# Layer 0 with row pairs in four classes: 32 x 64 products for two row pairs at once, and mirrored edges without VectorE's shuffles

## The chip, the cores and the metric

The kernel is one launch on one NeuronCore of a Trainium2 chip. The metric is the device time of that launch in microseconds (us); lower is better. Times of single executions are from the hardware profiler. The engines are called TensorE (PE; its weight loads are listed as PEld), VectorE (DVE), ScalarE (ACT), GpSimd (POOL) and SyncE (SP); an engine's name with a q is its instruction queue, which also issues transfers (DMAs).

## What is computed

Four layers follow one another on an f32 input x of 4 images x 16 channels x 512 x 512. Each is `x = x + conv(groupnorm(x))`. Only layer 0 is changed. Cut to what matters:

```python
def block(x, w1, b1, w2, b2, w3, b3, a, b, c):
    # each channel t with its neighbours t-1, t+1 (mirrored at the ends) as 3 input planes
    trip = stack([x[:, prev], x, x[:, nxt]], axis=2).reshape(B * T, 3, H, W)
    o = a * conv_reflect(trip, w1, b1, dil=1, pad=2) \
      + b * conv_reflect(trip, w2, b2, dil=2, pad=4) \
      + c * conv_reflect(trip, w3, b3, dil=4, pad=8)      # 5 x 5 taps each, reflected edges
    return tanh(o).reshape(B, T, H, W)

x = x + block(block(groupnorm(x), blk1...), blk2...)      # layer 0
```

So layer 0 convolves twice, and each convolution reaches 8 rows and 8 columns in every direction. Layers 1 (3 x 3 convolution on quantised data), 2 (17 x 17 box filter) and 3 (a complex 3 x 3 convolution between two Fourier transforms) read what layer 0 leaves in a DRAM tensor x1, in the same layout before and after the change.

## The kernel before

**Work in groups and slots.** Layer 0 walks through 32 groups: 4 images x 2 convolutions x 4 groups of 4 frames (a frame is one channel of one image, in the layout of a convolution's input). The three input planes of four frames are combined as in a fast convolution along the channels: `early` and `late` (lines 488 to 525) form six combinations of six neighbouring frames, each multiplied with its own set of weights, and `gather` puts six products together into four outputs. One product set is one *slot*: 32 x 6 = 192 slots. `slot` (line 684) writes out the order of the work by hand, for every engine: in slot p TensorE computes product set p, VectorE and ScalarE gather set p-1, form later combinations, apply tanh and finish earlier frames, and SyncE issues the transfers (`transfers`, line 212: the loads of y first, then other loads, then stores, spread over the slot by marks on the products). `later` puts a step into a later slot. The engines work through their own instructions in the order in which `slot` emits them.

**Layout.** A frame is a tile of 128 partitions x 2376 elements. A partition holds a pixel position of 16 columns x 2 rows within a block of the image; the free axis runs over blocks of columns and over row pairs. A product contracts 32 partitions (2 rows x 16 columns) to 32 outputs (again 2 x 16). A tap that reaches other rows is a shift by a number of row pairs, from -4 to 4; `DELTA` lists the seven that occur. Two blocks of columns (e = 0, 1) reach all columns. So there are 7 x 2 = 14 products per output, summed in PSUM.

**`products` (line 529).** For each of the 14 it makes 16 calls, one for each 32 x 32 tile of the array (i: the 32 partitions that are contracted; j: the 32 PSUM partitions that are written), 512 columns each. The moving operand is 8 blocks x 64 consecutive row pairs, shifted by `DELTA`. PSUM has two tiles of 4 banks: while one set is computed, the other is read by `gather`.

**Frames.** `x_frame` (line 412) normalises x on ScalarE and transposes it in 32 x 32 blocks on VectorE. `activated` (line 602) writes the tanh of the first convolution to a tile y, with mirrored edge rows made by a ScalarE multiplication with a parity mask (line 622) and a VectorE sum (in `y_out`, line 625); `y_out` stores y to DRAM. `y_frame` (line 427) loads it again as a frame for the second convolution, in 16 transfers, and one slot later `mirror` swaps rows of the first and last column block with two VectorE shuffles over partitions (lines 449 and 450). `early` and `late` read the frame afterwards. `z_out` (line 636) transposes the second convolution's result, adds it to x, takes the maximum and the minimum of each partition (lines 648 and 651; layer 1 needs them) and stores x1. The sums for the next normalisation are ScalarE's (line 668). At an image's end ScalarE issues the stores of x1 itself (line 664).

**Weights.** `load_weights` (line 199) loads a new set of weights on ScalarE's queue when the convolution changes. A set has 14 blocks of 32 columns in the order of `DELTA`; the host arranges them by `DELTA` too.

Of the kernel before, what the change touches and what calls it, by code (L numbers as in the profile page):

```python
# [20 lines left out]
P = 128  # L21
# [7 lines left out]
PX = 32  # L29
DIL = (1, 2, 4)  # L30
DELTA = (-4, -2, -1, 0, 1, 2, 4)
# [89 lines left out]
class Layer0:  # L121
# [101 lines left out]
    def load_x(self, b, t, half, name):  # L223

        xt = self.pools["x"].tile([P, 2 * W], F32, name=f"{name}_{b}_{t}_{half}", tag="x")
        self.load_half(xt, b, t, half)
        return xt
# [184 lines left out]
    def x_frame(self, b, t, raws, ek, f):  # L412

        nc = self.nc
        fr = self.free.pop(0)
        v = fr.rearrange("p (k r) -> p k r", r=72)
        scale, bias, _ = self.gn[b]
        for h in range(2):
            raw = raws[h].rearrange("p (s w) -> p s w", s=2)
            xp = self.normalised(raw, scale[:, t : t + 1], bias[:, t : t + 1], f"{b}_{t}_{h}")  # L420
            nc.vector.transpose(v[:, :, 4 + h : 68 : 2], xp)  # L421
        rim = ek.rearrange("p k (e f m) -> p k e f m", e=2, f=4)
        for side in range(2):
            nc.scalar.copy(v[:, :, 68 * side : 68 * side + 4], rim[:, :, side, f, :])
        return fr

    def y_frame(self, t):

        nc = self.nc
        fr = self.free.pop(0)  # L430
        v, y = fr.rearrange("p (k r) -> p k r", r=264), self.y[t, :, :, 0:528]
        first, last = y[:, 0, 0:264], y[:, 3, 264:528]
        for c in range(4):
            at = PX * c
            lo, hi = slice(at, at + 16), slice(at + 16, at + PX)
            for to, src in ((v[lo, 1:9], y[hi]), (v[hi, 0:8], y[lo])):
                self.move(to.rearrange("p (a k) r -> p a (k r)", k=2), src, "first")
            if c > 0:
                self.move(v[lo, 0], last[at - 16 : at], "first")
            if c < 3:  # L440
                self.move(v[hi, 8], first[at + PX : at + PX + 16], "first")

        self.move(v[0:9:8, 0], first[16:25:8], "first")
        self.move(v[119:P:8, 8], last[103:112:8], "first")
        left = [16 + p + 8 - 2 * (p % 8) if p < 16 and p % 8 else p for p in range(PX)]
        right = [p - 16 + 6 - 2 * (p % 8) if p >= 16 and p % 8 < 7 else p for p in range(PX)]

        def mirror():
            nc.vector.stream_shuffle(v[0:PX, 0], v[0:PX, 0], left)
            nc.vector.stream_shuffle(v[96:P, 8], v[96:P, 8], right)  # L450

        self.later(1, mirror)
        return fr
# [5 lines left out]
    def fetch(self, gr, p):  # L459

        b, conv, g = gr["b"], gr["conv"], gr["g"]
        if g == 0:
            order = {0: (1, 2), 1: (4,), 2: (3,), 4: (5,)} if conv else {0: (1,), 1: (2,), 2: (4,), 3: (3,), 4: (5,)}
        else:
            order = {0: (2,), 1: (4,), 2: (3,), 4: (5,)} if conv else {0: (2,), 1: (4,), 2: (3,), 4: (5,)}
        for i in order.get(p, ()):
            if g == 3 and i == 5:
                continue
            t = 4 * g - 1 + i
            if conv:  # L470
                gr["d"][i] = self.y_frame(t)
                continue
            t0 = 0 if i == 1 else min(4 * g + 1, 12)
            rim = (self.rims_ahead.pop(t0, None) or self.load_rims(b, t0)) if i < 3 else None
            raws = None if (b, t) in self.held else [self.load_x(b, t, h, "xr") for h in range(2)]
            self.later(1, partial(self.made, gr, i, t, t0, rim, raws))
# [52 lines left out]
    def products(self, gr, p):  # L529
        nc, conv, q = self.nc, gr["conv"], ORDER[p]  # L530
        ps = self.psum.tile([P, 4, 512], F32, name=f"m{self.now}", tag="m")
        v = gr["v"][q].rearrange("p (k r) -> p k r", r=264 if conv else 72)
        w = self.w[q].rearrange("p (n o) -> p n o", o=PX)
        for n in range(NPB):
            e, dr = n // len(DELTA), DELTA[n % len(DELTA)]
            for turn in range(16):
                i, j = turn // 4, turn % 4
                rows = slice(PX * i, PX * i + PX)
                r0 = 4 + dr + (64 * j if conv else 0)
                k0 = e + (0 if conv else 8 * j)  # L540
                ins = nc.tensor.matmul(  # L541
                    ps[PX * j : PX * j + PX, i, :].rearrange("p (k r) -> p k r", r=64),
                    w[rows, n],
                    v[rows, k0 : k0 + 8, r0 : r0 + 64],
                    start=(n == 0),
                    stop=(n == NPB - 1),
                    skip_group_check=True,
                )
            self.marks.append(ins.ins)
        gr["m"][q] = ps  # L550

    def gather(self, gr, p):
# [9 lines left out]
        def part(h):  # L562

            if conv:
                return m.rearrange("p c (k r) -> p (c k) r", r=64)[:, :, h::2]
# [36 lines left out]
    def activated(self, gr, i, h, src):  # L602
# [8 lines left out]
        else:  # L611
            if h == 0:
                gr["out"][i, 0] = self.pools["rb"].tile([P, 8, 264], F32, name=f"y_{name}", tag="rb")
            z = gr["out"][i, 0]
            o = z[:, :, 4 + 128 * h : 132 + 128 * h].rearrange("p k (c r) -> p c k r", c=2)
            nc.scalar.activation(o, src.rearrange("p (c k r) -> p c k r", c=2, k=8), AF.Tanh, bias=bias)
            to, even, odd = (
                (z[:, :, 0:4], z[:, :, 8:4:-1], z[:, :, 7:3:-1])
                if h == 0
                else (z[:, :, 260:264], z[:, :, 259:255:-1], z[:, :, 258:254:-1])  # L620
            )
            nc.scalar.mul(to, even, self.parity[:, 0:1])
            gr["rim"].append((to, odd))

    def y_out(self, gr, i):
        nc = self.nc
        for to, odd in gr["rim"]:
            self.stt(to, odd, self.parity[:, 1:2], to)
        gr["rim"].clear()
        y = self.y[4 * gr["g"] + i, :, :, 0:528]  # L630
        z = gr["out"].pop((i, 0)).rearrange("p (a k) r -> p a (k r)", k=2)
        wait = 2 if i == 3 else 1
        for a in range(4):
            self.later(wait, partial(self.move, y[:, a], z[:, a], "stores"))

    def z_out(self, gr, i):
# [8 lines left out]
        def finish():  # L645
            for h in range(2):
# [4 lines left out]
                nc.vector.tensor_reduce(self.low[:, b, t, h : h + 1], xs[h], AX.X, ALU.min)  # L651
# [5 lines left out]
        def leave():  # L657
            to = self.x1[b, :, t, :].rearrange("(p T s) w -> T p s w", T=2, s=2)
            neg = self.gn[b][2][:, t // 2 : t // 2 + 1]
            junk = self.pools["sum"].tile([P, 1024], F32, name=f"junk_{b}_{t}", tag="E")  # L660
            for h in range(2):
                x = xs[h].rearrange("p (s w) -> p s w", s=2)
                if self.last_of_image:
                    nc.scalar.dma_start(to[h], x)
                for r in () if self.last_of_image else range(0, P, PX):
                    self.move(to[h][r : r + PX], x[r : r + PX], "stores")
# [17 lines left out]
    def slot(self, n, p):  # L684
# [22 lines left out]
        if cur:  # L707
            self.products(cur, p)
        if done:
# [28 lines left out]
    def begin(self, gr):  # L738
# [3 lines left out]
        else:  # L742
            self.y = scratch(self.k.dram, f"y_{b}", [C, P, 4, 536])

    def run(self):
        self.groups = [
            {"b": b, "conv": conv, "g": g, "d": {}, "v": {}, "m": {}, "out": {}, "rim": [], "xb": {}}
# [989 lines left out]
```

## Time and profile before

| | us |
|---|---|
| device time, three runs | 5312.73, 5320.9, 5336.15 (median 5320.9) |
| profiled execution, its span from the first instruction to the last | 5311.8 |
| layer 0 in it (first product at 61.1, last one at 3019.9) | 2959 |

The page gives no other time of the profiled execution than its span; the fastest of the three runs lies 0.9 us above it.

| engine | busy us | share of the span |
|---|---|---|
| PE | 5017.0 | 94% |
| PEld | 3644.6 | 69% |
| DVE | 4034.8 | 76% |
| ACT | 2490.1 | 47% |
| POOL | 6.9 | 0% |

How to read the profile: a group of instructions stands as line, engine, operation, output<-inputs, partitions x elements and count; then, after the bar, busy time in us and mean ns of one; then the idle time of the engine just before them and what ended most of it. Matmuls are pipelined, so their durations overlap, and their ends are modelled; the distance between their starts tells more than the duration. A stretch is a window of the span, in us from its start.

### The profile page before, as it was taken

How to read it: one execution, taken by the hardware profiler on the slowest of the kernel's cores; microseconds unless marked ns; L12 is line 12 of the kernel's file. 1: busy time of each engine (PE TensorE's matmuls, PEld its weight loads, DVE VectorE, ACT ScalarE, POOL GpSimd, SP SyncE). 2: the span in 40 equal slices, each digit the busy share in tenths (PEclk: the TensorE clock that was granted, in tenths of full speed). 3: DMA queues.
4: the chain of work that ended last, by engine and by line, in shares of the span. 5: the costliest groups of instructions: out<-in, count | busy, mean ns of one | idle time of the engine just before them, and what ended most of it. 6: DMA issues, size and time to landing. Idle time of an engine off the chain costs nothing.

```text
span 5311.8 us, 270483 instructions
## 1 busy us (share of the span) xinstructions
PE 5017.0 (94%) x125040; PEld 3644.6 (69%) x125040; DVE 4034.8 (76%) x4765; ACT 2490.1 (47%) x3955; POOL 6.9 (0%) x20
## 2 busy tenths in 40 slices
PE   5999998999999999989999799998999989999999
PEld 3766666866666766768767655656887867777776
DVE  8857989758988669887679865555555578888887
ACT  3533345543345533444123454544454446666665
POOL 0000000000000000000000000000000000000000
PEclk9999999999999999999999899999999989999999
DMA  6555555555545465543446477776766655555554
GB/s 187 160 145 154 145 153 152 158 150 141 139 148 169 140 164 138 148 133 120 107 121 158 130 225 226 237 222 203 232 215 205 215 158 143 144 149 149 144 143 120
DMA packets 445356, 861.49 MB, mean 162 GB/s; under 512 B 74304, under 2 KB 96704, under 8 KB 443968
## 3 DMA queue, kind: packets, MB, share of 16 engines
q1 hardware_dynamic: 417520, 800.16, 52.2%
q10 hardware_dynamic: 26704, 44.03, 2.5%
q8 instruction: 979, 16.04, 1.4%
q14 instruction: 153, 1.25, 0.1%
HBM read 503.87 MB, written 340.03 MB: 159 GB/s over the span
## 4 chain that ended last, share of the span: by engine, by line
PE 90%; DVE 5%; issue 3%; DMA 1%; ACT 1%; SPq 0%; ACTq 0%; POOL 0%; DVEq 0%; POOLq 0%
PE m L541 52%; PE l1p L992 10%; PE l2p L1099 8%; PE u L1567 4%; PE s L1508 4%; PE u L1508 4%; PE u L1530 2%; PE pt L1542 2%; DVE l2o L1139 2%; PE l2p L1150 1%; DVE st L1140 1%; PE pr L1552 0%; DVE frame L457 0%; SPq L208 0%; DMA l0w<-frame 0%
## 5 line engine op out<-in xcount | busy, mean ns | idle before, releaser
L541 PE MATMUL m<-frame,l0w 32*32 32x512 f32 x86016 | 2863.1, 605 | 157.4 <-issue 76.7
L541 PEld LDWEIGHTS m<-frame,l0w 32*32 32x32 f32 x86016 | 2069.1, 103 | 950.5 <-issue 366.6
L457 DVE SCALAR_TENSOR_TENSOR frame<-frame,frame 128x2376 f32<-128x2376 f32 x232 | 607.8, 2628 | 8.8 <-DMA x<-xb 0.6
L992 PE MATMUL l1p<-l1q,l_wt 32*32 32x512 f32 x12288 | 482.2, 599 | 71.3 <-DVE l1q L982 36.2
L992 PEld LDWEIGHTS l1p<-l1q,l_wt 32*32 32x32 f32 x12288 | 257.8, 103 | 241.7 <-issue 162.5
L1139 DVE TENSOR_TENSOR l2o<-l2x,l2p 128x512 f32<-128x512 f32 x256 | 172.8, 675 | 266.5 <-PE l2p L1099 266.5
L668 ACT ACTIVATE junk<-xb,neg 128x1024 f32<-128x1024 f32 x256 | 294.1, 1149 | 62.9 <-DMA l0w<-l0w 19.9
L1099 PEld LDWEIGHTS l2p<-k_c_band,l2y 128*128 128x128 f32 x2048 | 256.7, 190 | 75.8 <-issue 55.0
L1099 PE MATMUL l2p<-k_c_band,l2y 128*128 128x144 f32 (+1 forms) x2048 | 284.2, 292 | 6.1
L1128 ACT COPY l2y<-l2p 128x512 f32<-128x512 f32 x256 | 149.9, 586 | 283.3 <-PE l2p L1099 283.3
L1099 PE MATMUL l2p<-k_c_band,l2n 128*128 128x144 f32 (+1 forms) x2048 | 269.2, 292 | 14.1 <-ACT l2n L1117 10.7
L1099 PEld LDWEIGHTS l2p<-k_c_band,l2n 128*128 128x128 f32 x2048 | 262.7, 197 | 14.8 <-ACT l2n L1117 11.3
L1009 DVE BATCH_NORM_STATS2 l1st<-l1o 128x6 f32<-128x512 f32 x256 | 158.2, 681 | 140.0 <-ACT l1o L1007 140.0
L1007 ACT ACTIVATE l1o<-l1p,k_l_bias,l_osc 128x1024 f32<-128x1024 f32 x128 | 147.2, 1200 | 236.2 <-PE l1p L992 230.1
L1567 PE MATMUL u<-k_c_hil,zt 128*128 128x128 f32 x2048 | 255.9, 278 | 0.0
L574 ACT COPY C<-m 128x1024 f32<-128x1024 f32 x64 | 61.6, 1014 | 393.2 <-PE m L541 288.3
L1567 PEld LDWEIGHTS u<-k_c_hil,zt 128*128 128x128 f32 x2048 | 238.4, 192 | 2.1 <-issue 0.8
L421 DVE STREAM_TRANSPOSE frame<-xp 128x1056 f32<-128x1056 f32 x128 | 162.7, 1281 | 96.7 <-ACT xp L390 96.6
L1543 ACT COPY zt<-pt 128x512 f32<-128x512 f32 x256 | 131.4, 599 | 208.6 <-PE pt L1542 208.6
L1473 DVE TENSOR_TENSOR xc<-l3n,k_c_tab 128x2048 f32<-128x2048 f32 x64 | 146.7, 2293 | 107.2 <-ACT l3n L1457 107.2
L1586 DVE SCALAR_TENSOR_TENSOR l3o<-u,l3t 128x256 f32<-128x256 f32 x512 | 192.5, 427 | 22.2 <-ACT l3t L1578 19.5
L992 PE MATMUL l1p<-l1x,l_wt 32*32 32x512 f32 x4088 | 196.2, 597 | 0.0
(312 smaller groups left out, 6374.8 us busy)
## 6 DMA issues: line engine op xcount, KB each, us to landing
y<-y SPq DMA_DIRECT2D x256, 264.0 KB
frame<-y SPq DMA_DIRECT2D x512, 132.0 KB
x<-l1o SPq DMA_DIRECT2D x256, 256.0 KB
l2x<-x SPq DMA_DIRECT2D x64, 1024.0 KB
x<-l2o SPq DMA_DIRECT2D x64, 1024.0 KB
l3x<-x SPq DMA_DIRECT2D x256, 256.0 KB
out<-l3o SPq DMA_DIRECT2D x256, 256.0 KB
l1x<-x SPq DMA_DIRECT2D x252, 256.0 KB
```

Source lines behind the costliest of these rows:

```text
L421: nc.vector.transpose(v[:, :, 4 + h : 68 : 2], xp)
L457: self.nc.vector.scalar_tensor_tensor(o, x, f, y, ALU.mult, ALU.add)
L541: ins = nc.tensor.matmul(ps[PX * j : PX * j + PX, i, :].rearrange("p (k r) -> p k r", r=64), w[rows, n], v[rows, k0 : k0 + 8, r0 : r0 + 64 ...
L668: nc.scalar.activation(junk, xs[h], f, bias=neg, accum_out=self.out_sums[n][:, 2 * t + h : 2 * t + h + 1])
L992: ins = nc.tensor.matmul(ps[32 * j : 32 * j + 32, b, :], wt[rows, a, d], qs[v % 3][rows, k, d : d + W] if d < 3 else raws[v][rows, k], sta ...
L1009: nc.vector.bn_stats(st[b][:, u, :], o[:, b, :])
L1099: nc.tensor.matmul(ps[:, lo:hi], lhs[:, k, at : at + P], band[:, j : j + hi - lo], start=(k == 0), stop=(k == 3), skip_group_check=True,)
L1128: nc.scalar.copy(yts[i][:, wb, :], ps)
L1139: nc.vector.tensor_add(o[:, hb, :], xt[:, hb, :], ps)
L1508: nc.tensor.matmul(ps[b][32 * j : 32 * j + 32], f[rows, n, j, :], x[rows, j, :], start=(i == 0), stop=(i == 2 and tag == "s"), skip_group_ ...
L1567: nc.tensor.matmul(po[:, bass.ts(k, P)], zt[:, b, k ^ 1, :], hil[:, k, :], start=False, stop=(k == 3), skip_group_check=True,)
L1586: nc.vector.scalar_tensor_tensor(o[:, v].rearrange("p k u -> p u k"), po[:, HW:W].rearrange("p (u k) -> p u k", u=2), s, t.rearrange("p (u ...
```

## The change

1. **Products.** The row pairs of a frame are stored in four classes (a frame's row pairs are dealt out in turn) so that two neighbouring row pairs of the output can be computed by one call: 32 partitions are contracted to 64 outputs, with the weight blocks of two shifts side by side. `DELTA` is put in an order in which such pairs lie next to each other. Of the seven shifts, ten of fourteen uses per pair of outputs are made in five such wide calls (`PAIRS`); the other four are made in 32 x 32 calls as before (`ALONE`). Each slot has its wide calls in one run and its narrow ones in another, wide first in even slots and narrow first in odd ones. Per slot 80 + 64 = 144 calls stand where 224 stood. The moving operand is read in runs of 16 or 32 elements.
2. **Frames and y.** The transposes, copies and tanh write in the new order, and the DRAM scratch for y has a new layout; a y frame comes in 22 transfers instead of 16, a y store goes in four of 32 partitions with 8.4 KB each instead of four of 128 partitions with 2.1 KB each.
3. **Mirrored edges.** The two VectorE shuffles and the parity steps in `activated` and `y_out` go. The loads of y fetch mirrored column blocks. `mirror` now is six small ScalarE multiplications per y frame, one slot after the load, emitted right after the products and ahead of `gather` (`self.do("edges")`); four of them fill a small tile that VectorE adds to the frame later in the slot (`added`). A GpSimd memset clears the two edge columns of every y tile.
4. **The minimum** in `z_out` is a `tensor_scalar` with an accumulated minimum, written over zr, instead of a `tensor_reduce`.
5. **Transfers of xb and x1** go in four pieces of 32 partitions in the new order of rows, also where ScalarE issues one whole store now.

```diff
-DELTA = (-4, -2, -1, 0, 1, 2, 4)
+DELTA = (4, 2, 0, -2, -4, 1, -1)
+PAIRS = ((4, 0), (2, 1), (0, 2), (-2, 3), (1, 5))
+ALONE = (((-4, 4), (6, 0)), ((-1, 6), (3, 5)))
...
     def y_frame(...)
+        whole = self.y[t, :, :, 0 : 32 * 132].rearrange("u (h s j) (k n) -> h s j u k n", h=2, s=2, n=132)
+        y = whole[:, :, ::-1]
         for c in range(4):
...
+            first, last = 1 if c == 0 else 0, 8 if c == 3 else 9
+            for to, src in (
+                (v[lo, :, first:9], y[1, :, :, :, 8 * c - 1 + first : 8 * c + 8]),
+                (v[hi, :, 0:last], y[0, :, :, :, 8 * c : 8 * c + last]),
+            ):
+                for u in range(2):
+                    part = src[:, :, u].rearrange("s j k n -> s j (k n)")
+                    self.move(to[:, u].rearrange("p k n -> p (k n)"), part, "first")
...
         def mirror():
-            nc.vector.stream_shuffle(v[0:PX, 0], v[0:PX, 0], left)
-            nc.vector.stream_shuffle(v[96:P, 8], v[96:P, 8], right)
-        self.later(1, mirror)
+            for side, m, back in ((0, 1, odd), (65, 64, even)):
+                nc.scalar.mul(at(0, 0, side, 1188, 66), at(1, 1, m, -1188, -66), back)
+            nc.scalar.mul(edge[:, :, :, 0, 0], at(0, 0, 2, 1187), even)
+            nc.scalar.mul(edge[:, :, :, 0, 1], at(1, 1, 1, -1188), even)
+            nc.scalar.mul(edge[:, :, :, 1, 0], at(1, 0, 64, -1188), odd)
+            nc.scalar.mul(edge[:, :, :, 1, 1], at(0, 1, 64, 1187), odd)
+        def added():
+            to = fr.rearrange("p (n c m) -> p n c m", n=18, c=2)[:, :, :, 0:66:65]
+            nc.vector.tensor_add(to, to, edge.rearrange("p u k s c -> p (u k) c s"))
+        self.later(1, mirror, "edges")
+        self.later(1, added)
...
     def products(self, gr, p):
-        for n in range(NPB):
-            e, dr = n // len(DELTA), DELTA[n % len(DELTA)]
-            for turn in range(16):
-                i, j = turn // 4, turn % 4
-                ins = nc.tensor.matmul(ps[PX * j : PX * j + PX, i, :]..., w[rows, n], v[rows, k0 : k0 + 8, r0 : r0 + 64], ...)
+        runs = [(e, pair) for e in range(2) for pair in PAIRS], [(e, two) for e in range(2) for two in ALONE]
+        order = [(wide, *what) for wide in ((1, 0) if p % 2 == 0 else (0, 1)) for what in runs[1 - wide]]
+        for n, (wide, e, what) in enumerate(order):
+            base = len(DELTA) * PX * e
+            for i in range(4):
+                for j in range(2):
+                    if wide:
+                        d, o = what
+                        at = base + PX * o
+                        ins = product(slice(64 * j, 64 * j + 64), i, slice(at, at + 64), d, e, j, n)
+                        continue
+                    for u, (d, o) in enumerate(what):
+                        at = base + PX * o
+                        out = slice(64 * j + PX * u, 64 * j + PX * u + PX)
+                        ins = product(out, i, slice(at, at + PX), d, e, j, n)
...
     def activated(...)
+                nc.gpsimd.memset(gr["out"][i, 0][:, :, 0:66:65], 0.0)
...
-            nc.scalar.mul(to, even, self.parity[:, 0:1])
-            gr["rim"].append((to, odd))
     def y_out(self, gr, i):
-        for to, odd in gr["rim"]:
-            self.stt(to, odd, self.parity[:, 1:2], to)
...
     def z_out(...)
-                nc.vector.tensor_reduce(self.low[:, b, t, h : h + 1], xs[h], AX.X, ALU.min)
+                nc.vector.tensor_scalar(
+                    zr[:, h], x, 1.0, None, ALU.mult, ALU.min, accum_out=self.low[:, b, t, h : h + 1]
+                )
...
     def slot(self, n, p):
         if cur:
             self.products(cur, p)
+        self.do("edges")
         if done:
             self.gather(done, at)
```

`product` is the same matrix product call, with a moving operand of three levels: blocks, two classes, and 32 (second convolution) or 16 (first) row pairs of each class.

## The prediction

> **What bounds the kernel now.** I read the page first: the chain of work that ended last, then the costliest groups. The changed layer is the first 3020 of 5311.8 us, and the chain lies on TensorE.
>
> ```profile
> PE 90%; DVE 5%; issue 3%; DMA 1%; ACT 1%; SPq 0%; ACTq 0%; POOL 0%; DVEq 0%; POOLq 0%
> ...
> L541 PE MATMUL m<-frame,l0w 32*32 32x512 f32 x86016 | 2863.1, 605 | 157.4 <-issue 76.7
> L541 PEld LDWEIGHTS m<-frame,l0w 32*32 32x32 f32 x86016 | 2069.1, 103 | 950.5 <-issue 366.6
> ```
>
> The reader is to see that the products of layer 0 (L541) keep TensorE busy for 2863 us and that each of the 32 groups x 6 slots x 224 calls stands there twice (86016 = 192 x 448): an f32 product runs as two passes, each with its own weight load. Then I read the table of stretches for one image, cut at its eight groups (four of the first convolution, four of the second). Columns: stretch, length, busy time of PE, PEld, DVE, ACT and POOL, clock, DMA share, GB/s.
>
> ```profile
> 808.70:913.20 104.50, 93.52 (x2691) 64.83 (x2695) 98.36 (x90) 61.91 (x106) 0.00 (x0) 0.91 0.52 155
> 913.20:998.70 85.50, 85.50 (x2703) 73.50 (x2686) 70.23 (x55) 51.58 (x98) 0.00 (x0) 1.00 0.52 164
> 998.70:1084.60 85.90, 85.90 (x2708) 72.97 (x2689) 65.50 (x51) 48.74 (x87) 0.00 (x0) 1.00 0.47 146
> 1084.60:1179.20 94.60, 91.75 (x2707) 60.74 (x2697) 51.76 (x57) 30.86 (x50) 0.00 (x0) 1.00 0.61 153
> 1179.20:1269.70 90.50, 89.30 (x2706) 61.81 (x2687) 67.73 (x78) 24.60 (x33) 0.80 (x2) 1.00 0.54 148
> 1269.70:1362.90 93.20, 91.51 (x2704) 57.90 (x2690) 88.95 (x85) 33.47 (x45) 0.00 (x0) 1.00 0.60 145
> 1362.90:1453.40 90.50, 89.72 (x2715) 61.34 (x2694) 81.97 (x75) 31.27 (x44) 0.00 (x0) 1.00 0.52 136
> 1453.40:1552.30 98.90, 90.10 (x2704) 65.10 (x2687) 79.52 (x73) 46.34 (x80) 0.00 (x0) 0.99 0.51 154
> ```
>
> Stretches 2 and 3 are pure TensorE: 85.9 us for 6 x 448 pairs of load and matmul, 32 ns a pair, 14.3 us a slot. Stretch 1 and stretches 6 to 8 are held almost as much by VectorE (79.5 to 98.4 us busy). Stretch 4, where the first convolution hands over to the second, has both engines partly idle.
>
> **TensorE: the term that decides.** Per slot the change makes 10 wide products per 32 rows by 64 columns tile (80 calls on 8 tiles) and 4 narrow ones per 32 by 32 tile (64 calls on 16 tiles): 144 calls, 288 pairs, where 448 stood. The multiplications stay the same: each tile still streams 14 products of 512 columns. So the gain hangs on whether a pair or a stream is the limit. Today 14 rounds of 16 tiles take 14.3 us, 1.02 us a round. What a bare stream takes shows in layer 3, where L1530 works on two tiles of 64 rows, again 512 columns in f32 (timeline, start and length in us):
>
> ```profile
> 4426.45 1.59 PE L1508 MATMUL u<-xs,f 32*32 32x512 f32 x26
> 4427.97 1.99 PE L1530 MATMUL u<-cor,lc 64*128 64x512 f32 x8
> 4429.89 0.33 PE L1542 MATMUL pt<-k_c_ident,z 128*128 128x128 f32 x1
> ```
>
> Eight passes start over 1.40 us (1.99 less the 0.59 of the last one, the median of this line) with one 0.11 us of first weights in it: three steps of 0.43 us, two passes at a time. A product of two passes thus streams in 0.86 us, and its loads of 128 columns (186 ns each) are hidden. Layer 0 needs 1.02, so 0.16 us a round are not streaming. The likeliest cause is the number of pairs in flight: L1508 takes the same tiles in another order (four row blocks first, then the next column block) and starts 87 passes in the 3.00 us from 4421, 34 ns each, so the order of tiles matters little and the count of instructions much.
>
> Wide part: from below 10 x 0.86 = 8.6 us, the stream; from above 10 x 1.02 = 10.2, no gain. I take 8.6, because L1530 is the only row with tiles wider than 32 columns, and its loads were twice as long as 64 columns need. Narrow part: 4 x 1.02 = 4.1. New per slot: one change of tile shape. No such change stands between 32 by 32 and 32 by 64 in the trace; the nearest is L1508 to L1530 above, where the last start before lies 0.52 us ahead of the first after it and the first weights take 0.11 more. From below 0.1 (weights alone), from above 0.62; I take 0.35. Sum 8.6 + 4.1 + 0.35 = 13.05 us against 14.3: **1.2 us a slot, 7.2 us a group**, wherever TensorE alone is the limit. Ends: 8.6 + 4.1 + 0.1 saves 1.5; 10.2 + 4.1 + 0.62 costs 0.6. The moving data now come in runs of 16 or 32 elements rather than 64; L541's runs of 64 and L1508's of 512 go alike, so I cost that at 0.
>
> The Trainium skill speaks against this part twice. Its page TensorEngine Tiling (Array Packing), Key Properties, says that changing the tiling mode drains TensorE; it gives no figure. TensorE: Matmul & The Clock Gate, Part 3, says that a weight load overlaps running matmuls only where its row group differs; by that rule a wide tile's longer loads would stay exposed and the slot would keep its 14.3 us. L1530 differs: with two row groups, both always streaming, its loads cost nothing after the first, so the trace decides.
>
> **VectorE.** The rows it rests on:
>
> ```profile
> L651 DVE TENSOR_REDUCE low<-xb 128x1 f32<-128x1024 f32 x128 | 156.1, 1220 | 4.4
> ...
> L457 DVE SCALAR_TENSOR_TENSOR y<-y,k_c_parity 128x32 f32<-128x32 f32 x128 | 30.7, 249 | 180.7 <-ACT y L622 152.6 <-DMA xr<-in_x 14.6 <-DMA l0w<-l0w 12.4
> L450 DVE STREAM_SHUFFLE frame<-frame 32x264 f32<-32x264 f32 x64 | 29.0, 453 | 2.0
> L449 DVE STREAM_SHUFFLE frame<-frame 32x264 f32<-32x264 f32 x64 | 28.1, 440 | 0.8 <-issue 0.6
> ...
> L519 DVE TENSOR_SCALAR frame<-frame 128x2376 f32<-128x2376 f32 x8 | 11.1, 1390 | 0.0
> ```
>
> Gone: 128 shuffles (57.1 us) and 128 parity sums (30.7). New: 64 small additions of 128x72; the 128x64 product of L1491 took 225 ns, so 64 x 0.24 = 15. The minimum becomes a TENSOR_SCALAR that accumulates: as a plain one by L519 (1390 ns for 2376 elements) 0.60 us for 1024, plus the 82 ns read-out that L648 shows, 0.68; as slow as the reduction plus read-out, 1.30. I take 0.68, the same operation's row: 128 x 0.54 = 69 us less (other end: 10 more). In a second-convolution group that is 8 x 0.54 + 4 x 0.89 - 4 x 0.24 = **6.9 us** (1.9 at the other end); in a first-convolution group 8 x 0.25 = 2.0.
>
> **ScalarE, GpSimd, SyncE.** ScalarE gives up 128 multiplications of 325 ns (42 us) and takes 384 of 36 elements; L389's 128x16 took 206 ns and L622's 128x32 325, so 80 to 125 us, 1.2 to 2.0 us in a slot that loads a frame. It was busy 25 to 33 us of 90 in those groups, so the work itself costs nothing; if that cover were gone, it would be 80 us. Its place does matter: these now stand ahead of the PSUM copies and wait for the frame's loads (rival below). The 64 memsets on GpSimd (busy 6.9 us in all) stand before the first tanh, which waits for the same buffer anyway: 0, at most 0.2 us each by the 128x128 memset of L812. A y frame takes 22 transfers where 16 stood, 384 more on SyncE's queue; the 32 of two frames from 342.5 us took 25.1 us there, 0.78 each, for twice the bytes that most of the new ones carry. Bytes are the same and pieces longer (4.2 to 8.4 KB for 2.1). I cost it at nothing except in stretch 4, where that queue already runs behind. The stores of x1 and the loads of xb keep pieces of 4 KB and their number, but for the 64 whole stores that ScalarE issues at an image's end: they become 256 quarters. The one at 1499.64 us took 0.46 us to issue, so between 0 and 192 x 0.46 = 88 us, hidden in stretches 8 and 1, where ScalarE is busy 46 of 99 and 62 of 104 us.
>
> **The sum, by group of an image.** Stretches 2, 3 and 5 are TensorE's, VectorE stays below 71: 7.2 each. Stretch 4: half, 3.6, as transfers share it. Stretches 6 and 7: VectorE lets go of at most 6.9; I take 5 each. Stretch 8 ends in VectorE work: 4. Stretch 1 likewise: 3. Together 42.2 us; four images 169. 5311.8 - 169 = 5143 for the profiled execution. The three runs lie 0.9, 9.1 and 24.4 us above its span, the median 9.1, so **5150 us** for the median.
>
> **Rivals.** (a) TensorE gains, but it is given back: the low minimum stays at 1.30 us, stretches 6 and 7 give 1.5 each, 1 and 8 nothing, and stretch 4 nothing: 24.6 an image, 98; with some waits of ScalarE on loads 80: **5240**. For it: VectorE's 89 of 93.2 us in stretch 6.
>
> (b) The round of 1.02 us belongs to streaming 16 tiles' worth of output, not to the count of pairs. Then a slot is 14.3 + 0.35; stretches 2, 3 and 5 lose 2 each, 6 to 8 gain 1 to 2 from VectorE: about +2 an image, **5330**, no change. For it: nothing shows a 32 by 64 tile. Against it: L1530.
>
> (c) Slower: ScalarE waits. It runs in order, the mirrored edges now stand ahead of the copy of the finished products, and their loads can be late (waits in layer 0):
>
> ```profile
> DVE frame L449 <- DMA frame<-y: 113.2, 16, 10.5
> ```
>
> Today VectorE met this late in the slot, 16 times of 64. At the head of the slot ScalarE meets it 5 to 15 us sooner. The other half of PSUM gives TensorE one slot of patience, so it decides only where a load lands over about 11 us into the slot after the one that issued it; the two frames of stretch 4 do (their queue ran to 367.7, the slot began at 355.4). If every one of the 64 frames cost 4 us, 256 - 169 = 87: **5400**.
>
> **Chances.** Forecast 0.53; (a) 0.20; (b) 0.11; (c) 0.16. Range 5080 (1.5 us a slot and all 6.9 us of VectorE: 52 an image, 207; and 36% of the 77 us that PE waited on issue, 28, for 36% fewer instructions) to 5340, which takes in (a) and (b) and leaves out (c) and a little below: 0.8. A difference under 0.5% can't be told from no change here. Faster by over 0.5%: 0.53 + 0.20 - 0.01 = 0.72; within: 0.12; slower: 0.16.
>
> **What will show it.** Right: in stretches 2 and 3 a group of about 79 us with wide passes about 53 ns apart (8.6 us for 160), one gap under 0.6 us at each change of shape, the minimum at 0.68 us. Wrong: wide passes 64 ns apart (rival b), or ScalarE's copies of L574 waiting for frame<-y with TensorE idle behind them (c).

## The result, and the profile after it

The changed kernel takes 6271.31 us (median of 4 runs, 6269.15 to 6273.69), beside 5316.81 us (4 runs) of the kernel before: a ratio of 1.1793, 95% interval 1.1768 to 1.1818. It is **slower by 18%**. The forecast was 5150 us; 5340, the top of the range, is 930 us too low.

The page of the profiled execution (span 6271.9 us), first its chain of work that ended last, by engine, and then groups of instructions:

```profile
PE 63%; DMA 16%; DVE 10%; issue 4%; SPq 3%; ACT 3%; ACTq 0%; DVEq 0%; POOL 0%
...
L579 PE MATMUL m<-frame,l0w 32*64 32x512 f32 (+1 forms) x55296 | 2730.2, 636 | 1269.6 <-ACT C L626 579.7
L579 PEld LDWEIGHTS m<-frame,l0w 32*64 32x64 f32 (+1 forms) x55296 | 1173.4, 123 | 2825.5 <-issue 1635.4
L471 ACT ACTIVATE frame<-frame,k_c_parity 128x36 f32<-128x36 f32 x128 | 39.3, 355 | 1414.8 <-DMA frame<-y 523.2
```

Transfers hold 16% of the chain where they held 1%. The products have 55296 passes instead of 86016 and TensorE is busy with them for less time than before, but it idles 1269.6 us ahead of them instead of 157.4, and 924 us of that idle time end with a copy of ScalarE (L626, which empties a PSUM tile; 579.7 and 344.1 us for its two tiles). ScalarE in turn idles 1415 us ahead of its mirrored edges (L471); 523 of them, the largest part, are put down to loads of y, and 641 to transfers of xb and x1 that share the queue with them.

The table of stretches for the same image (stretch, length, busy time of PE, PEld, DVE, ACT and POOL with counts, clock, DMA share, GB/s):

```profile
1064.60:1180.30 115.70, 90.28 (x1735) 37.08 (x1743) 105.44 (x94) 63.25 (x107) 0.38 (x2) 0.86 0.49 142
1180.30:1270.60 90.30, 82.23 (x1736) 36.75 (x1728) 70.68 (x46) 45.54 (x78) 0.76 (x4) 0.94 0.48 148
1270.60:1362.80 92.20, 82.35 (x1741) 36.89 (x1732) 72.07 (x45) 47.21 (x82) 0.75 (x4) 0.93 0.44 139
1362.80:1524.60 161.80, 85.23 (x1737) 36.97 (x1729) 46.80 (x33) 33.59 (x65) 0.74 (x4) 0.77 0.23 78
1524.60:1684.60 160.00, 89.39 (x1739) 35.78 (x1731) 60.45 (x60) 30.64 (x56) 1.17 (x4) 0.77 0.24 83
1684.60:1821.80 137.20, 85.84 (x1736) 36.67 (x1728) 83.90 (x77) 37.68 (x68) 0.00 (x0) 0.80 0.32 100
1821.80:1954.50 132.70, 83.77 (x1736) 36.74 (x1728) 83.54 (x77) 39.54 (x70) 0.00 (x0) 0.82 0.35 105
1954.50:2065.50 111.00, 86.07 (x1737) 36.68 (x1721) 88.90 (x85) 47.79 (x81) 0.00 (x0) 0.90 0.48 135
```

The image takes 1000.9 us where it took 743.6. Of the 257 us that are lost, 223 are in stretches 4 to 7, which load the frames of y (stretches 2 to 5 store them): stretch 5 needs 160 us instead of 90.5. There no engine is busy for more than 90 us of 160, and the transfers move less, not more: 83 GB/s at a DMA share of 0.24, where 148 and 0.54 stood. So the time is lost to transfers that are slow without being many.

Where they are slow shows in SyncE's queue (timeline: start and length of a run of issues). First the kernel after, then the kernel before, each in its second convolution:

```profile
1698.34 23.18 SPq L219 DMA_DIRECT2D frame<-y  x22
1722.66 4.41 SPq L219 DMA_DIRECT2D x<-xb  x8
1727.16 23.09 SPq L219 DMA_DIRECT2D frame<-y  x22
```

```profile
1271.64 10.53 SPq L217 DMA_DIRECT2D frame<-y  x16
1282.28 5.66 SPq L217 DMA_DIRECT2D x<-xb  x8
1288.03 12.07 SPq L217 DMA_DIRECT2D frame<-y  x16
```

A frame here keeps the queue for 23 us instead of 11 to 12, for 22 transfers instead of 16. A product slot lasts 13 us. Over all 64 frames it is 22.8 to 31.9 us (24.9 in the middle), where it was 10.5 to 17.3 (12.3). ScalarE's row at the same place (timeline; in brackets the idle time and its releaser) shows what stands behind it:

```profile
1725.07 0.61 ACT L471 ACTIVATE frame<-frame,k_c_parity 128x36 f32<-128x36 f32 x2 [22.97 <-DMA frame<-y]
...
1726.44 1.90 ACT L626 COPY A<-m 128x1024 f32<-128x1024 f32 x2
```

The edges wait 23 us for the load, and the copy that frees PSUM waits behind them. The DMA columns of two windows of this kernel, one over loads of xb and one over the frame loads, say what kind of slowness it is:

```profile
1688.40:1698.20 9.80, 9.64 (x224) 3.94 (x208) 6.32 (x9) 6.88 (x12) 0.00 (x0) 1.00 0.74 193
1698.40:1721.40 23.00, 13.50 (x288) 5.62 (x288) 22.86 (x20) 3.63 (x6) 0.00 (x0) 0.88 0.17 59
```

At 0.17, fewer than 3 of the 16 DMA engines are at work. In the packet records of the second window packets of 4752 bytes take 184 ns each and run two at a time (16.7 of 17.5 us); the stores of y, packets of 8448 bytes, run four at a time (18.8 of 20.5 us from 1270). The diff has these numbers: a load of 16 rows is written as two steps of eight rows (`s j`, s = 2, because j is stored and read backwards, which leaves the mirrored pieces in plain order), a store of 32 rows as four steps of eight (`u q j n`, q = 4).

### The profile page after: what moved, and what is told of

Same layout as the page of the kernel before. It is cut to its first block, busy times and chain, and to the rows that moved or that the text cites. A ratio compares the mean times of both kernels' runs of the same rounds, so it can differ in the third digit from the quotient of the medians.

```text
span 6271.9 us, 210181 instructions
## 1 busy us (share of the span) xinstructions
PE 4879.1 (78%) x94320; PEld 2747.2 (44%) x94320; DVE 4064.1 (65%) x4573; ACT 2555.3 (41%) x4211; POOL 18.6 (0%) x84
## 4 chain that ended last, share of the span: by engine, by line
PE 63%; DMA 16%; DVE 10%; issue 4%; SPq 3%; ACT 3%; ACTq 0%; DVEq 0%; POOL 0%
PE m L579 31%; DMA frame<-y 12%; PE l1p L1037 9%; PE l2p L1144 6%; PE u L1612 4%; PE s L1553 4%; PE u L1553 3%; SPq L219 3%; PE u L1575 2%; PE pt L1587 2%; DVE frame L487 2%; DVE frame L428 1%; DVE l2o L1184 1%; DMA xr<-in_x 1%; PE l2p L1195 1%
## 5 line engine op out<-in xcount | busy, mean ns | idle before, releaser
L579 PE MATMUL m<-frame,l0w 32*64 32x512 f32 (+1 forms) x55296 | 2730.2, 636 | 1269.6 <-ACT C L626 579.7
L579 PEld LDWEIGHTS m<-frame,l0w 32*64 32x64 f32 (+1 forms) x55296 | 1173.4, 123 | 2825.5 <-issue 1635.4
L471 ACT ACTIVATE frame<-frame,k_c_parity 128x36 f32<-128x36 f32 x128 | 39.3, 355 | 1414.8 <-DMA frame<-y 523.2
L487 DVE SCALAR_TENSOR_TENSOR frame<-frame,frame 128x2376 f32<-128x2376 f32 x232 | 607.9, 2629 | 8.9 <-PE m L579 0.5
L479 DVE TENSOR_TENSOR frame<-frame,edge 128x72 f32<-128x72 f32 x64 | 15.9, 248 | 880.3 <-ACT edge L475 553.7
L428 DVE STREAM_TRANSPOSE frame<-xp 128x1056 f32<-128x1056 f32 x128 | 259.3, 2109 | 50.4 <-ACT xp L397 50.4
L691 DVE CUSTOM_DVE_ANT_0 xb<-xb,zr 128x1024 f32<-128x1024 f32 x128 | 156.2, 1220 | 140.3 <-DMA xb<-in_x 140.2
```

What stands on the lines that cost most here:

```text
L428: nc.vector.transpose(v[:, :, :, h, 1:17].rearrange("p k u m -> p k m u"), xp)
L487: self.nc.vector.scalar_tensor_tensor(o, x, f, y, ALU.mult, ALU.add)
L579: return nc.tensor.matmul(ps[at, i, :].rearrange("p (k c m) -> p k c m", k=nc_, c=2), w[PX * i : PX * i + PX, weights], source(i, d, e, j) ...
L691: nc.vector.tensor_tensor_reduce(x, x, zr[:, h], 1.0, -3.0e38, ALU.add, ALU.max, self.top[:, b, t, h : h + 1])
```

## The experiments

**Theory A**: a transfer runs on as many DMA engines as its outermost step has entries, 2 for the new loads and 4 for the new stores, and that is the loss. **Rival B** is the prediction's slower case: the loads are late anyway, and ScalarE's edges ahead of the copies make TensorE pay. **Rival C**: the new products or the layout in classes are slow. Each ratio below is to the kernel before as it ran on the same occasion (5295.63, 5313.76, 5317.45 or 5308.63 us); where runs of two occasions are compared, the difference by their ratios stands in brackets.

### The shape of the transfers

`e1_rows16` keeps products, frames and edges, and stores y with its rows in plain order, so that loads have one step of 16 rows and stores one of 32. The mirrored column blocks, for which the order was reversed, go to a small tensor ye of their own (four more small stores a frame; four of the 22 loads read it).

```diff
-        y = whole[:, :, ::-1]
+        y = whole
...
+        rows = self.y[t, :, :, 0 : 32 * 132].rearrange("u (h p) (k n) -> h p u k n", h=2, n=132)
...
-                    part = src[:, :, u].rearrange("s j k n -> s j (k n)")
+                    part = src[:, u].rearrange("p k n -> p (k n)")
...
-        y = self.y[4 * gr["g"] + i].rearrange("u (q j) n -> u q j n", j=8)[:, :, ::-1]
+        y = self.y[4 * gr["g"] + i]
...
+            to = self.ye[4 * gr["g"] + i, r % 2, side].rearrange("(q j) n -> q j n", j=8)[:, ::-1]
...
+            self.later(wait, partial(self.move, to, part, "stores"))
```

> The changed kernel, with y kept in DRAM in plain row order, so that a load or store of y names its 16 or 32 rows in one step instead of 2 steps of 8 or 4 steps of 8; the mirrored column blocks get a small scratch of their own (4 more small stores per frame). Theory A (the transfers of y run on as many DMA engines as their outermost step has entries, two for loads): a frame's 22 loads fall from 23 us to 12 to 15 us, packets of 4752 bytes run up to 16 at a time, the waits between slots fall from 1290 us to under 300, and the time comes to 5100 to 5350 us. Theory B (ScalarE's mirrored edges ahead of the PSUM copies are the cause, however fast the loads): 5900 to 6300 us. Theory C (wide products or the changes of tile shape are slow): unchanged, 6270.

Measured: 5287.01 us, ratio 0.9975 (0.9959 to 0.9992). The whole loss is gone, 984 us (965) with one change in how the same bytes are addressed. A frame's 22 loads keep the queue for 12.2 us in the middle. A window over one frame's loads, in the kernel before and in e1_rows16:

```profile
1288.00:1300.10 12.10, 12.10 (x385) 8.43 (x374) 12.00 (x10) 10.26 (x16) 0.00 (x0) 1.00 0.51 113
```

```profile
1195.00:1206.60 11.60, 11.60 (x317) 6.24 (x306) 2.13 (x11) 8.14 (x11) 0.59 (x2) 1.00 0.52 133
```

`e2_loads16` has only the loads in the new form, `e3_stores16` only the stores; in both the rows land in another order within eights, so only their times count.

> The changed kernel with only the 16 large loads of a y frame in one step of 16 rows; the stores stay in 4 steps of 8 rows, so the rows of a y frame land in the wrong order within eights and the output is not the reference's. Theory A: the loads are most of the loss; the second convolution's groups fall from 155 to about 85 us, 5250 to 5450 us in all. Theory B: above 5900. Theory C: 6270.

> The changed kernel with only the stores of y in one step of 32 rows; the loads stay in 2 steps of 8, so rows are in the wrong order within eights and the output is not the reference's. Theory A: the loads still take 23 us a frame; only the waits of 9 to 11 us in the third slot of the first convolution's groups go, 6050 to 6200 us. Theories B and C: 6270.

Measured: 5455.0 us (ratio 1.0284, 1.0251 to 1.0318) and 5992.66 us (1.1298, 1.1261 to 1.1335). So with quick loads the stores on four engines still cost 168 us, and with quick stores the loads on two still cost 706, each beside e1_rows16 on the same occasion.

`e8_before_two` makes the counter-test in the kernel before, which has neither wide products nor ScalarE's edges (again with rows in another order):

```diff
...
-                self.move(to.rearrange("p (a k) r -> p a (k r)", k=2), src, "first")
+                self.move(to.rearrange("p k r -> p (k r)"), src.rearrange("(m s) a n -> s m (a n)", s=2), "first")
...
-            self.y = scratch(self.k.dram, f"y_{b}", [C, P, 4, 536])
+            self.y = scratch(self.k.dram, f"y_{b}", [C, P, 4 * 528 + 16])
```

> The kernel before, where only the main loads of a y frame are changed: the y tensor in DRAM has its four pieces of a row next to each other, and a load of 16 rows is written as two times eight rows (every second row; so rows arrive in the wrong order and the output is not the reference's). Bytes, number of transfers, products, shuffles stay. If a transfer runs on as many DMA engines as its outermost step has entries, the 1.08 MB of a frame's main loads take about 18 us at the 59 GB/s of the changed kernel instead of 10.5 to 12 us, VectorE's shuffles and combinations come late, and the kernel before itself is slower by 300 to 900 us: 5600 to 6200. Rival: only the class layout or the small pieces of the changed kernel are slow: 5317, within 1%.

Measured: 5817.8 us, ratio 1.0956 (1.0936 to 1.0975): 504 us more. Its stretches 4 and 5 and a window over one frame's loads:

```profile
1210.40:1343.00 132.60, 94.31 (x2708) 73.11 (x2694) 50.46 (x51) 26.47 (x42) 0.00 (x0) 0.83 0.31 100
1343.00:1465.30 122.30, 92.21 (x2707) 66.01 (x2697) 67.44 (x81) 28.97 (x40) 0.80 (x2) 0.87 0.36 116
...
1404.00:1420.00 16.00, 16.00 (x524) 12.39 (x508) 3.52 (x5) 0.00 (x0) 0.00 (x0) 1.00 0.17 63
```

The DMA share is again 0.17, at 63 GB/s, packets of 8448 bytes run two at a time (13.2 of 14.0 us), and stretches 4 and 5 grow from 94.6 and 90.5 us to 132.6 and 122.3. Theory A holds in a kernel without any other part of the change. (In it the y tensor's pieces also lie closer together, so that packets are longer; that edit was not run alone.)

### The place of ScalarE's edges

`e4_edges_late` is the changed kernel with the edges emitted where VectorE's shuffles stood; `e7_um_late` and `e13_pool_late` make the same edit in kernels with quick loads.

```diff
-        self.later(1, mirror, "edges")
+        self.later(1, mirror)
```

> The changed kernel with ScalarE's mirrored edges emitted late in the slot, where VectorE's shuffles were, instead of ahead of the PSUM copies; loads as in the change. Theory A: the queue still needs 23 us a frame, 38 with the other transfers of a frame, so four frames keep a group of the second convolution above 125 us; some of the waits go, 5800 to 6150 us. Theory B: the waits behind the PSUM copies go and with them nearly all of the loss, 5200 to 5450 us. Theory C: 6270.

Measured: 6248.29 us, ratio 1.178 (1.1738 to 1.1822), against 1.1793. Waits (engine, line, waited for: us in total, times, longest; "issue" is nothing that the profile shows) of the changed kernel, then of e4_edges_late:

```profile
PE m L579 <- ACT C L626: 579.7, 20, 40.6
PE m L579 <- ACT A L626: 344.1, 21, 34.5
DVE frame L479 <- ACT edge L475: 553.7, 28, 32.7
```

```profile
PE m L579 <- issue: 675.8, 38, 38.2
DVE frame L479 <- ACT edge L475: 644.5, 35, 60.5
PE m L579 <- DVE frame L487: 229.8, 25, 23.7
PE m L579 <- ACT C L626: 171.5, 16, 26.3
PE m L579 <- ACT A L626: 60.1, 7, 15.9
```

The wait has only moved. TensorE's idle time that ends with a copy falls from 924 to 232 us, but all its idle time ahead of the products hardly does (1238.5 us for 1269.6); VectorE's additions wait longer for the edges, and the combinations behind them (L487) now hold up TensorE. A late load reaches TensorE either way, so B's order is not the cause. With quick loads the order makes no difference either: see e7_um_late beside e6_um and e13_pool_late beside e12_pool below.

### The products

`e5_narrow` is e1_rows16 with every wide product written as two narrow ones.

```diff
-        runs = [(e, pair) for e in range(2) for pair in PAIRS], [(e, two) for e in range(2) for two in ALONE]
+        alone = [((d, o), (d, o + 1)) for d, o in PAIRS] + list(ALONE)
+        runs = [], [(e, two) for e in range(2) for two in alone]
```

> e1_rows16 with all fourteen products of a slot as 32 x 32 calls (224 calls a slot as before the change, and no change of shape inside a slot); frames, transfers, edges and minimum stay those of e1_rows16. If the wide calls are what saves 12.78 to 13.28 against 14.3 us a slot, the slot goes back to 14.3 us and stretch 2 of an image from 80.0 to about 86; stretches that already wait absorb part, so 100 to 200 us are lost: 5390 to 5490. Rival 1: the saving comes from something else in the new layout (no wide call needed): the slot stays near 13 and the time near 5287. Rival 2: the moving data in runs of 16 and 32 elements cost something of their own: slot well over 14.3, over 5500.

Measured: 5434.99 us, ratio 1.0231 (1.0211 to 1.0251): the wide calls are worth 148 us (136 by the ratios). Stretches 2 and 3 of one image, e5_narrow and then e1_rows16:

```profile
958.00:1044.80 86.80, 86.80 (x2705) 73.05 (x2691) 73.29 (x46) 47.89 (x83) 0.76 (x4) 1.00 0.61 162
1044.80:1132.20 87.40, 87.17 (x2705) 75.18 (x2686) 69.54 (x44) 47.04 (x79) 0.75 (x4) 1.00 0.55 147
```

```profile
928.80:1008.80 80.00, 80.00 (x1736) 36.86 (x1728) 70.94 (x46) 45.70 (x78) 0.75 (x4) 1.00 0.60 167
1008.80:1090.20 81.40, 79.67 (x1736) 36.21 (x1728) 72.06 (x45) 46.69 (x82) 0.75 (x4) 1.00 0.61 163
```

TensorE is busy almost throughout in both, and the groups are 6.8 and 6.0 us apart. C is out: the products gain what they should.

### What else keeps the gain small

In e1_rows16 TensorE's gain is there, but waits take it back: from first to last start of their passes the slots of layer 0 hold 2590 us instead of 2857, and between them lie 363 us instead of 102. Of the 262 us more, four images together, 56 are in stretch 1, 52 in stretch 4 and 43 in stretch 8; stretches 1 and 8 are longer than before the change (112.7 and 107.5 us against 104.5 and 98.9). One candidate is VectorE: its transposes of x take 2109 ns in the changed kernel and took 1281 (groups; the changed kernel, with the minimum as second row, then before):

```profile
L428 DVE STREAM_TRANSPOSE frame<-xp 128x1056 f32<-128x1056 f32 x128 | 259.3, 2109 | 50.4 <-ACT xp L397 50.4
L694 DVE TENSOR_SCALAR_CACHE_REDUCE zr<-xb 128x1024 f32<-128x1024 f32 x128 | 156.1, 1220 | 4.4
```

```profile
L421 DVE STREAM_TRANSPOSE frame<-xp 128x1056 f32<-128x1056 f32 x128 | 162.7, 1281 | 96.7 <-ACT xp L390 96.6
```

`e6_um` sorts the rows of x by class as they are loaded, so that a transpose writes 16 elements in a row rather than single ones 36 apart:

```diff
-            nc.vector.transpose(v[:, :, :, h, 1:17].rearrange("p k u m -> p k m u"), xp)
+            nc.vector.transpose(v[:, :, :, h, 1:17], xp)
...
-        src = self.a["x"][b, t].rearrange("(p T s) w -> T p (s w)", T=2, s=2)[half]
-        n = PX if self.marks else P
-        for r in range(0, P, n):
-            self.move(xt[r : r + n], src[r : r + n])
+        src = self.a["x"][b, t].rearrange("(J m u T s) w -> T J u m (s w)", J=4, m=16, u=2, T=2, s=2)[half]
+        for r in range(8):
+            self.move(xt[16 * r : 16 * r + 16], src[r // 2, r % 2])
```

> e1_rows16 with x loaded so that the rows of one class lie in 16 neighbouring partitions (eight transfers of 16 rows per half frame instead of four of 32): the transposes of the first convolution's frames then write runs of 16 elements next to each other instead of single elements 36 apart. If the write pattern is what made them 2.11 instead of 1.28 us, they go back to about 1.28 us, VectorE has 128 x 0.83 = 106 us less, and stretches 1 and 8 (105 of 113 and 87 of 107 us busy) shorten by 5 to 10 us an image: 30 to 80 us less than e1_rows16, 5205 to 5255. Rival: the transposes are slow for another reason (a collision with other engines or transfers): they stay near 2.1 us and the time near 5287, or a little above it for 4 us more of issuing on SyncE per frame.

> e6_um with ScalarE's mirrored edges moved from ahead of the gather copies to the place where VectorE's shuffles stood. In e1_rows16 those copies came late behind edges that waited 337 us in all for the last pieces of a frame (DMA frame<-ye). If that order costs time once the loads are quick (the mechanism of rival c at a smaller price), 15 to 60 us less than e6_um: 5160 to 5230. If the wait is hidden, no difference to e6_um within 10 us.

Measured: 5520.78 us (ratio 1.0391, 1.0372 to 1.041) and 5520.83 (1.0393). The transposes did what was expected, the time did not:

```profile
L427 DVE STREAM_TRANSPOSE frame<-xp 128x1056 f32<-128x1056 f32 x128 | 162.4, 1275 | 127.3 <-ACT xp L396 127.3
```

So the pattern of the write sets their duration, but the new loads cost more than it saves: e6_um takes 234 us more than e1_rows16 (221), and moving the edges in it changes nothing. `e10_xr_only` does it only where the data are transposed, so that SyncE issues fewer:

```diff
-            self.load_half(xt, b, t, half)
+            self.load_half(xt, b, t, half, name == "xr")
...
```

> e1_rows16 with the rows of x sorted by class inside each block of 32 partitions as in e6_um, but only for the loads that are transposed (xr); the loads that only feed the sums of the next image (xs) keep their four transfers. In e6_um the transposes went to 1.28 us as meant, but its SyncE issued 32 transfers for every frame of the first convolution, some 0.47 us each, 15 us a slot. If that full queue is what cost 230 us there, it now holds 24 of them, 11.3 us a slot, which fits into a slot of 13 us: time below e1_rows16 by 30 to 80 us, 5205 to 5255. Rival: pieces of 4 KB from every second row are slow to load by themselves: time stays well above 5287, 5350 to 5450.

Measured: 5373.35 us, ratio 1.0095 (1.0076 to 1.0114): 147 less than e6_um (157), still 86 more than e1_rows16 (64). My expectation failed. 31 us of it stand at the start: the first frames now come in 96 transfers, and the first product starts at 94.5 us instead of 63.1. Stretch 1, in e1_rows16 and then in e10_xr_only:

```profile
816.10:928.80 112.70, 87.15 (x1733) 36.65 (x1741) 105.32 (x94) 63.27 (x107) 0.38 (x2) 0.88 0.53 149
```

```profile
859.20:973.00 113.80, 90.27 (x1728) 37.09 (x1736) 99.40 (x95) 63.69 (x108) 0.37 (x2) 0.86 0.54 148
```

It takes 113.8 us though VectorE is busy 99.4 of it instead of 105.3, and over four images TensorE waits no less between the slots of stretches 1 and 8 (123 and 63 us; 118 and 59 in e1_rows16). So quicker transposes did not shorten these stretches, and what holds them is not shown. Whether the rest is the queue or the pieces from every second row was not settled.

`e11_pool_queue` takes e10_xr_only and lets GpSimd issue the eight small transfers of ye; `e12_pool` makes this edit alone in e1_rows16, and `e13_pool_late` adds the late edges.

```diff
+        for to, src in self.moves["side"]:
+            self.nc.gpsimd.dma_start(to, src)
...
```

> e10_xr_only with the eight small transfers of mirrored column blocks per frame (four stores, four loads of ye) issued by GpSimd instead of SyncE. SyncE has 64 x 8 x about 0.55 us = 280 us less to issue, and the edges of a frame no longer wait behind its main loads and other stores. If SyncE's queue is what the slots of the hand-over (stretch 4 and the starts of the second convolution) wait for, 20 to 60 us less than e10_xr_only. Rival: GpSimd's queue stands behind its memsets, which wait for tanh buffers, so that loads come later: 0 to 60 us more than e10_xr_only.

> e1_rows16 with the eight small transfers of mirrored column blocks per frame issued by GpSimd instead of SyncE (the edit of e11_pool_queue alone, without sorted rows of x). There it took 68 us off. If SyncE's queue is what the starts of the second convolution wait for, the same 40 to 80 us come off e1_rows16: 5205 to 5245, a version faster than both kernels. Rival: those 68 us were only the queue that the extra loads of x had filled; then e1_rows16 is changed by less than 15 us.

> e12_pool with ScalarE's mirrored edges emitted after the gather copies, where VectorE's shuffles stood. In e11_pool_queue these edges still waited 167 us for frame<-y at the head of a slot. If that delays the copies and so TensorE, 10 to 40 us less than e12_pool; if the other half of PSUM covers it, no difference within 10 us; if the additions of VectorE now wait in their turn, up to 20 us more.

Measured: 5305.08 us (0.9977, 0.9965 to 0.9989), **5235.81 us** (0.9868, 0.9851 to 0.9885) and 5236.26 (0.9872, 0.9851 to 0.9893). SyncE's queue was worth 68 us in e10_xr_only and 51 in e1_rows16 (57). In this edit the small transfers are also no longer tied to marks on the products, so queue and time of issue changed together. The late edges of e13_pool_late make no difference. e12_pool beats both kernels, by 1.3% against the one before. Stretches 3 to 6 of e12_pool, which in e1_rows16 took 81.4, 97.6, 89.7 and 87.1 us:

```profile
994.30:1075.10 80.80, 79.78 (x1741) 36.41 (x1733) 72.41 (x45) 47.10 (x83) 10.03 (x20) 1.00 0.60 167
1075.10:1167.60 92.50, 82.67 (x1736) 37.83 (x1728) 47.11 (x34) 38.99 (x77) 22.30 (x40) 0.94 0.70 164
1167.60:1252.80 85.20, 82.80 (x1736) 42.34 (x1728) 63.55 (x64) 29.11 (x53) 19.75 (x37) 0.98 0.69 156
1252.80:1335.40 82.60, 80.57 (x1736) 36.69 (x1728) 80.30 (x72) 37.70 (x68) 8.74 (x16) 1.00 0.67 164
```

The gain is in the stretches that load y (4 to 6, and 7 with 85.7 instead of 89.5), as a shorter queue would have it.

## Why the prediction was wrong

**The step that failed** is the one on ScalarE, GpSimd and SyncE: "A y frame takes 22 transfers where 16 stood ... Bytes are the same and pieces longer ... I cost it at nothing except in stretch 4". It counted transfers, bytes and lengths of pieces, and left out how many DMA engines a transfer uses. A frame went from some 12 us to 23 and more, longer than a slot, in all 64 frames, and this alone cost 706 us; the stores, too, were costed at nothing and took 168 us by themselves. Together they cost 984 us, against 169 us of forecast gain. The rearrangements in the diff showed the two and the four.

The Trainium skill has the rule: DMA: Bandwidth & Descriptors, in the section on why a DMA increments its semaphore by 16 and not by 1, says that the number of engines is the largest one up to 16 that divides the length of the slowest step longer than 1 on both sides. The runs agree: 2 by 8 rows against 16 partitions ran two packets at a time, 4 by 8 against 32 ran four, and a step of 16 rows lifted the rate over a frame's loads from 59 to 133 GB/s. Reading the new access patterns by it would have shown that these transfers had to stand in the sum.

**TensorE** was right. Undisturbed slots take 12.83 us where the wide part comes first and 13.28, with 0.41 more to the next slot, where it comes last: 13.27 on average, against 13.05 forecast and 14.3 before. The parts are 8.4 us (8.6) for 160 wide passes, 3.9 to 4.4 (4.1) for the narrow ones, and 0.54 us (0.35) between the last start of one shape and the first of the other, of which a wide group's usual pause is 0.4. So the longer weight loads of the wide tiles do not hold the slot at 14.3 us. By e5_narrow a group in stretch 2 gains 6.8 us (7.2). The wide passes start 53 ns apart on the mean, but in bursts of eight with a pause of 0.38 to 0.41 us. In the changed kernel layer 0 has 211 us less from first to last start within its slots (2646 against 2857) and 1188 more between them (1290 against 102).

**VectorE** was half right. Shuffles and parity sums went, and the 64 additions cost 15.9 us (15). The minimum takes 1220 ns as the reduction did and 83 ns for its read-out, not 0.68 us: the other end of that bound held, and 69 us of expected relief did not come. The transposes were not costed at all, although the diff changes where they write: 97 us more in place of nothing.

**ScalarE's edges** take about 118 us (39.3 for L471 and 256 others at 0.31), within the 80 to 125 forecast, and they do wait at the head of a slot, as rival (c) had it: 523 us in 23 frames for frame<-y, and in 28 more the profile names transfers of xb and x1 around them. But a queue behind in stretch 4 was not the reason for late loads, the price of 4 us a frame was too low (1188 us more between slots are 18.6 for each of 64 frames), and the place of the edges was no part of it: e4_edges_late.

**The sum.** With quick transfers (e1_rows16) stretch 2 gives 5.5 us and stretch 3 4.5 of the 7.2 forecast, 5 to 7 give 0.8, 6.1 and 1.0, but 4, 1 and 8 lose 3.0, 8.2 and 8.6 where they were to gain 3.6, 3 and 4. In the image shown that is a loss of 1.9 us instead of a gain of 42.2. In e12_pool it is a gain of 16.7. So even without the failed step the forecast was too high. VectorE's slower transposes and its full-length minimum fall in the stretches that it nearly fills, but that they are the reason is not shown: with quick transposes (e10_xr_only) stretch 1 got no shorter, and the minimum was not changed alone.

## What to carry to other kernels

For each transfer that a change rewrites, write down the outermost step of both sides as well as bytes and count: a reversal or a split that makes it 2 leaves most DMA engines idle, and in a profile it looks like a low DMA share with a full queue behind it. A strided write can slow an instruction whose shape is unchanged, so moved outputs belong in the sum. And a gain of one engine reaches the time only where the transfers that feed it fit into its new, shorter slot.

## What the runs showed of the hardware

- Windows over the loads of a frame, all transfers in them counted, show 59 to 64 GB/s where 16 rows are written as two steps of eight, and 133 GB/s where they are one step of sixteen. Packets ran two at a time in the first form, up to sixteen at a time in the second.
- A transpose of 128x1056 elements took 1275 to 1281 ns when it wrote runs of 16 or single elements two apart, and 2109 ns when it wrote single ones 36 apart.
- A wait costs more than its length. In the changed kernel the 58 slots that begin after a wait of over 5 us take 15.0 us, instead of 12.8 where the wide part comes first and 13.3 where it comes last, and in stretches 4 to 7 the granted clock is 0.77 to 0.82 instead of 1.00. The clock records of this trace hold only 0.5 and 1.0, and all 58 slots begin at 0.5, which lasts for 3.0 to 6.2 us more (4.6 in the middle). After the wait of 17 us that ends at 1728.4, 40 passes run in the first 4 us and 80 in the next 4:

```profile
1728.40:1732.40 4.00, 4.00 (x40) 1.43 (x48) 2.98 (x4) 3.97 (x5) 0.00 (x0) 0.50 0.13 44
1732.40:1736.40 4.00, 4.00 (x80) 1.43 (x72) 3.93 (x4) 2.92 (x6) 0.00 (x0) 0.95 0.13 53
```

The page TensorE: Matmul & The Clock Gate of the Trainium skill, Part 1, has the array at half clock after an idle window of some 3.4 us, until about as long a busy one has passed. The trace agrees: 1.7 to 2.2 us lost a slot would be 3.5 to 4.4 us at half clock, an estimate, beside the 4.6 recorded.
